# Four cross-attention layers on one core: setup work moved inside layer 0, attention 1's first rows moved into layer 0's FFN, and layer 2's raw weights issued by ScalarE's queue

## The chip, the cores and the metric

The kernel runs on one core of a Trainium2 chip. The core has five engines that work side by side, each with its own instruction stream: TensorE (PE, matrix products and transpositions; its weight loads are shown apart as PEld), VectorE (DVE), ScalarE (ACT), GpSimd (POOL) and SyncE (SP, which here only issues DMAs). An engine runs its instructions in order and waits on semaphores for the others. DMAs move data between HBM and the on-chip memories; the matrix products' results land in PSUM, whose banks the other engines copy out.

The metric is the device time of one execution in microseconds. Three runs of the kernel before gave a median of 1427.58 us.

## What is computed

x has the shape (4, 256, 256), ctx (4, 512, 128), all in fp32. There are four layers, each a cross-attention of x to ctx followed by a feed-forward part; both are added to x. Cut to what matters here:

```
layer 0 attention: q = LN((x Wq + bq) by heads), k = LN((ctx Wk + bk) by heads), 16 heads of 16,
                   a second set of 16 keys from the last rows of ctx (Wkv_dca), softmax each,
                   sum of both contexts, times Wo, plus bo
layer 0 FFN:       64 "arrows" (A: 16 rows each); per token the 4 of the largest norm are routed;
                   out = x W^T + (routed arrows) B + bias
layers 1 to 3 attention: xn = LN(x); 16 query heads of 128, 8 key/value heads of 128,
                   softmax(xn Wq (ctx Wk)^T / sqrt(128)) ctx Wv Wo, masked by mask_BxS2
layer 1 FFN:       8 experts, two per token, plus a shared expert (SwiGLU)
layer 2 FFN:       two experts and a gate
layer 3 FFN:       64 tokens of a sequence are chosen, the rest pass by
```

The kernel folds the weights of the attentions of layers 1 to 3 beforehand: for each head m = Wq Wk^T / sqrt(128) and n = Wv Wo, so that queries are multiplied with ctx directly.

## The kernel before

The batch (B = 4) is the outer loop of each attention; rows are tiled by 128 (P), so a batch has NC = 2 chunks of queries and NK = 4 chunks of keys. x stays on chip in `x_sb[b]` through the whole kernel.

On PE, ACT, DVE and POOL the program's order is written out by hand: within a block each of these engines issues its instructions in the order in which the source emits them. The functions are therefore cut into small steps, and the loops call steps of the next piece of work between the steps of the present one. SP, which isn't in that list, issues DMAs as they come.

**Layer 0's attention** (to about 150 us) goes through b = 0 to 3, and for each batch through i = 0 to 7: four scores of a group of heads (`scores`, L1333, ps L1340), the values of the group before (`values`, L1350), and then `between(b, i)` (L1543), which prepares batch b + 1: its layernorm and projections, the normalisation of q and k by heads (class Scale: the small steps hv L1232, hr L1237 on ACT, he L1241 and pad L1244 on DVE), and their transpositions (`transposed`, L1305: pT L1315 on PE, copies to kT and qT on DVE L1327 and ACT L1329). `between` also holds work that is done once in the kernel:

- `bias_rows` (L1280, two additions on DVE), `bias_columns` (L1288: four tiny matmuls pbrow L1291, a DVE copy L1295) and `output_bias` (L1297: four matmuls pbo L1300, an addition on DVE L1301): they carry the values' bias through Wo into the output's bias `bo0`, which `output0` (L1392) adds; `output0(0)` comes at b = 1, i = 6.
- `score_bound` (L1264): seven DVE operations on one partition, whose result is read only when the kernel decides at its end whether its bounds held.
- the mask: `mf` (L1587, a DVE copy), `pmk` (L1591, one transposition on PE), `mbias` (L1592, DVE), for attention 1.
- `quad` (L1597 to L1601): four DVE operations that make a constant for later attentions.

The values' bias rows lie in a tile `brow` (L1050), loaded by DMA at the start; it has the tag "kT" in the pool w0, two buffers, which the tiles kT of the batches share.

**Layer 0's FFN** (F0, L1658 to L1696, about 150 to 235 us) runs over n = 0 to 7, chunks of 128 rows (b = n / 2). Class Arrows has for each n four steps: `vectors` (paf L1424, ACT copies), `routes` (L1435 to L1453: eight operations on DVE and a product `twof` on POOL), `turned` (puTf L1461 on PE, copies on ACT) and `output` (pyf L1470 and L1474 on PE, ysf L1476 on DVE, the sum into x on POOL). Between them `folding(1, ...)` (L974) is called, eight steps over the loop, each with products pm (L985) and pn (L1001) on PE, scaling and squares on ACT (L993, L996) and a copy n_sb on DVE (L1004). PSUM is one pool here, `ring`, which is closed after the loop; the pool `psum` takes its banks.

`routes` of chunk n + 2 is called at the start of turn n, with one exception: for n = 5 the call stands behind the turn's output and its two fold steps.

**Attention 1** (`attention`, L1719) begins with the layernorm of batch 0's rows, unless it is given as `first_xnT`: `Norm` (L908: statistics on DVE, a power on POOL), `tokens` (L925) and `layernorm_T` (L937: four transpositions pxn, then an ACT copy L940). Then `first_queries` (pq L1803) starts the products.

**Layer 1's FFN** (F1) runs 23 blocks of 128 gathered rows from about 600 to 655 us. The loop over j calls for block j + 2 `gather` (an indirect DMA by POOL) and `turn_in` (pxg L2344 on PE, copy xgT L2346 on ACT), for j + 1 `rise` (pgu L2369 on PE, sigmoids sg L2374 and L2375 on ACT, products gT on DVE) and for j `fall` (pyr L2387). For every second j the two blocks are finished (`last_rows`, L2393) and stored: `yr` (L2398, ACT, three buffers), from which a DMA on SP's queue (L2401) writes `yd` in HBM. Inside this loop the raw weights of attention 2 are loaded by `load_raw` (L958, DMA at L969), a quarter each at the end of j = 1, 5, 9 and 13, held back until the last yr before it (`done["slots"]`). A quarter is four DMAs: 512, 128, 128 and 512 KB. `folding(2, ...)` uses them after the loop.

## Time and profile before

| what | value |
|---|---|
| three runs, median (lowest to highest) | 1427.58 us (1425.8 to 1429.04) |
| profiled execution, its own time | 1426.74 us |
| its span on the core | 1424.9 us |
| mean granted TensorE clock | 0.997 |
| PE busy | 1401.6 us |
| DMA, whole kernel | 46.82 MB, mean 33 GB/s |

The profile page cuts the span into 40 slices of 35.6 us. In the row of PE a 9 is 90% or more of the slice; the row of GB/s shows where transfers crowd: the 18th slice, 605 to 641 us, reaches 217 GB/s:

```
PE   9999999999999999999999999999999999999998
ACT  5667454433433332255443333333454333333331
PEclk9999999999999999999999999999999999999999
GB/s 163 2 1 2 75 75 1 86 27 1 8 0 8 1 8 22 53 217 91 49 56 8 16 1 1 8 1 9 117 106 48 16 1 1 1 1 1 1 1 33
```

Some of the DMA issues (line, queue, count, size of each, median time from issue to landing):

```
wq<-in_L_wqT SPq DMA_DIRECT2D x11, 512.0 KB, 5.1
wo<-in_L_wo SPq DMA_DIRECT2D x11, 512.0 KB, 7.4
yd<-yr SPq DMA_DIRECT2D x23, 128.0 KB, 4.9
```

In a row of a timeline the first number is the start in us from the span's start, the second the time to the end of the group, then engine, line, operation, tiles out<-in, shapes and count; in brackets stands the engine's idle time just before and what ended it.

### The profile page before, as it was taken

The page shows a single profiled execution, that of the slowest core. Times are in us where ns is not written, and L with a number is a line of the kernel's source. Part 1 is how long each engine was busy: PE and PEld are TensorE (multiplying, and loading weights), DVE is VectorE, ACT ScalarE, POOL GpSimd, SP SyncE. Part 2 cuts the span into 40 slices and gives each one's busy share as a digit, 9 for nine tenths or more (in the row PEclk, how much of TensorE's full clock was granted, in tenths as well). Part 3 has the DMA queues.
Part 4 walks back from the last instruction along what each step waited for, and adds up shares of the span by engine and source line. Part 5 has one row for each costly group of instructions (what it writes and reads, how often), then busy time and mean ns, then how long its engine had stood idle before and what let it go on. Part 6 is the DMA issues. An engine that isn't in the chain of part 4 may idle for free. (4 is left out here: it accounts for less than half of the span.)

```text
span 1424.9 us, 20263 instructions
## 1 busy us (share of the span) xinstructions
PE 1401.6 (98%) x7393; PEld 927.0 (65%) x7393; DVE 896.7 (63%) x2012; ACT 590.2 (41%) x1168; POOL 679.2 (48%) x812
## 2 busy tenths in 40 slices
PE   9999999999999999999999999999999999999998
PEld 7566676566556667887555666665985556666666
DVE  6666863666665557554676565648755666575675
ACT  5667454433433332255443333333454433333331
POOL 3322332475655455231566656566214765445560
PEclk9999999999999999999999999999999999999999
DMA  5000220300000000272120000000331000000000
GB/s 163 2 1 2 75 75 1 86 27 1 8 0 8 1 8 22 53 217 91 49 56 8 16 1 1 8 1 9 117 106 48 16 1 1 1 1 1 1 1 33
DMA packets 49449, 46.82 MB, mean 33 GB/s; under 512 B 8281, under 2 KB 45242, under 8 KB 49340
## 3 DMA queue, kind: packets, MB, share of 16 engines
q1 hardware_dynamic: 45740, 37.29, 8.6%
q0 software_dynamic: 2496, 6.82, 1.8%
q8 instruction: 61, 1.00, 0.3%
q10 hardware_dynamic: 1104, 1.31, 0.3%
q14 instruction: 48, 0.39, 0.1%
HBM read 38.60 MB, written 6.82 MB: 32 GB/s over the span
## 5 line engine op out<-in xcount | busy, mean ns | idle before, releaser
L1870 POOL TENSOR_TENSOR half<-pT 128x1024 f32<-128x1024 f32 x93 | 218.2, 2347 | 290.7 <-ACT pT L1854 215.6
L1851 PE MATMUL ps<-qT,cT 128*128 128x512 f32 x768 | 345.6, 593 | 0.0
L1859 PE MATMUL po<-pT,c_sb 128*128 128x512 f32 x768 | 345.3, 592 | 0.0
L1854 ACT ACTIVATE pT<-ps,mbias 128x512 f32<-128x512 f32 x384 | 263.7, 687 | 155.9 <-PE ps L1851 141.6
L1859 PEld LDWEIGHTS po<-pT,c_sb 128*128 128x128 f32 x768 | 145.8, 190 | 183.2 <-issue 183.2
L1851 PEld LDWEIGHTS ps<-qT,cT 128*128 128x128 f32 x768 | 138.9, 190 | 138.4 <-issue 136.5
L1863 ACT COPY oT<-po 128x512 f32<-128x512 f32 x96 | 56.2, 586 | 265.0 <-PE po L1859 265.0
L1906 POOL TENSOR_TENSOR oT<-oT,wide 128x512 f32<-128x512 f32 x90 | 114.3, 1290 | 17.3 <-DVE wide L1905 17.3
L1831 DVE TENSOR_TENSOR qT<-qT,paq 128x128 f32<-128x128 f32 x90 | 25.4, 283 | 94.9 <-ACT qT L1830 94.9
L1344 ACT ACTIVATE pT<-ps 128x512 f32<-128x512 f32 x128 | 65.9, 604 | 32.6 <-PE ps L1340 32.4
L1878 DVE TENSOR_TENSOR half<-half 128x512 f32<-128x512 f32 x96 | 71.6, 746 | 2.7 <-POOL half L1868 2.5
L1831 DVE TENSOR_TENSOR w<-w,pao 128x128 f32<-128x128 f32 x21 | 6.0, 286 | 106.5 <-ACT w L1830 106.5
L1880 DVE STREAM_TRANSPOSE turned<-half 128x512 f32<-128x512 f32 x96 | 68.3, 712 | 6.3
L1821 PE MATMUL paq<-xnT_a,m_sb 128*128 128x128 f32 x360 | 71.3, 280 | 0.0
L1821 PE MATMUL paq<-xx,m_x 128*128 128x128 f32 x360 | 69.6, 275 | 0.0
L1821 PEld LDWEIGHTS paq<-xnT_a,m_sb 128*128 128x128 f32 x360 | 57.3, 192 | 17.2 <-issue 8.7
L1884 DVE TENSOR_REDUCE sums<-turned 128x16 f32<-128x512 f32 x96 | 65.9, 686 | 3.3
L1821 PE MATMUL pao<-n_x,ox 128*128 128x128 f32 x336 | 65.2, 276 | 0.3 <-POOL ox L1747 0.3
L1830 ACT COPY qT<-paq 128x128 f32<-128x128 f32 x90 | 23.9, 265 | 94.1 <-PE paq L1821 94.1
L1905 DVE STREAM_TRANSPOSE wide<-rz 128x512 f32<-128x512 f32 x96 | 62.2, 685 | 0.1
L1834 DVE TENSOR_TENSOR qT<-qT,pbq 128x384 f32<-128x384 f32 x90 | 49.9, 554 | 9.4
L1821 PEld LDWEIGHTS paq<-xx,m_x 128*128 128x128 f32 x360 | 54.7, 192 | 0.0
(454 smaller groups left out, 2589.2 us busy)
## 6 DMA issues: line engine op xcount, KB each, us to landing
wq<-in_L_wqT SPq DMA_DIRECT2D x11, 512.0 KB, 5.1
wo<-in_L_wo SPq DMA_DIRECT2D x11, 512.0 KB, 7.4
yd<-yr SPq DMA_DIRECT2D x23, 128.0 KB, 4.9
w<-in_F_w SPq DMA_DIRECT2D x4, 512.0 KB, 3.6
xd<-xn_f SPq DMA_DIRECT2D x7, 256.0 KB, 2.2
wk<-in_L_wkT SPq DMA_DIRECT2D x11, 128.0 KB, 5.2
wv<-in_L_wvT SPq DMA_DIRECT2D x11, 128.0 KB, 5.6
x_sb<-in_x SPq DMA_DIRECT2D x4, 256.0 KB, 3.1
```

What stands on the lines that cost most here:

```text
L1344: nc.scalar.activation(pT[kp][:, j], ps[j], AF.Exp)
L1821: nc.tensor.matmul(p[:, at, :], lhsT=lhsT, rhs=rhs, start=(k == 0 and at == 0), stop=(k == len(of) - 1 and i == which[-1]),)
L1851: nc.tensor.matmul(ps, lhsT=cT[:, b, k * P : (k + 1) * P], rhs=qT, start=True, stop=True)
L1854: nc.scalar.activation(pT[:, k, :], ps, AF.Exp, bias=mbias[:, b, k : k + 1])
L1859: nc.tensor.matmul(po, lhsT=c_sb[:, b, k, :], rhs=pT[:, k], start=(k == 0), stop=(k == NK - 1))
L1863: done["head"] = nc.scalar.copy(raw, po).ins
L1870: nc.gpsimd.tensor_tensor(half, pT[:, 0:2], pT[:, 2:4], ALU.add)
L1878: nc.vector.tensor_tensor(part, half[:, 0], half[:, 1], ALU.add)
L1880: nc.vector.transpose(turned.rearrange("p f i -> p (f i)"), part)
L1884: nc.vector.tensor_reduce(sums[b, hp // 4][:, hp % 4, :], turned, AX.X, ALU.add)
L1905: nc.vector.transpose(wide, rzs[b, hp // 4][:, hp % 4, :, None].to_broadcast([P, NB, 32]))
L1906: eng.tensor_tensor(outs[b, hp], outs[b, hp], wide.rearrange("p f i -> p (f i)"), ALU.mult)
```

## The change

Four edits are joined.

1. In layer 0's `between`, `bias_rows`, `bias_columns` and `output_bias` go from b = 0, i = 0, 1, 4 to b = 1, i = 0, 1, 2; `score_bound` from b = 0, i = 3 to b = 3, i = 2; the mask from b = 1, i = 0, 1 to b = 3, i = 0, 1; `quad` from b = 1, i = 6 to b = 3, i = 3.
2. In F0 `routes` of chunk 7 is called at its normal turn, at the start of n = 5.
3. Attention 1's first layernorm moves into F0's loop: `Norm` at the end of n = 5, `tokens` at the end of n = 6, `layernorm_T` at n = 7 between the output and the last fold step; `attention(1, ...)` is given the result.
4. `load_raw` takes a queue, and the four loads for layer 2 are issued by ScalarE: 16 DMA instructions that were in SP's stream are in ACT's.

```diff
-    def load_raw(L, i, after=None, tiles=None):
+    def load_raw(L, i, after=None, tiles=None, queue=None):
...
-            dma = nc.sync.dma_start(dst, src[a * P : (a + z) * P, :].rearrange("(h e) d -> e h d", e=P))
+            dma = (queue or nc.sync).dma_start(dst, src[a * P : (a + z) * P, :].rearrange("(h e) d -> e h d", e=P))
...
-            if b == 0:
+            if b == 1:
                 if i == 0:
                     bias_rows()
                 elif i == 1:
                     bias_columns()
-                elif i == 3:
-                    score_bound()
-                elif i == 4:
+                elif i == 2:
                     output_bias()
-            if b == 1:
+            if b == B - 1:
                 if i == 0:
 
                     mf = w0.tile([B * NK, P], F32, tag="hs", name="mf", bufs=1)
...
-                elif i == 6:
+                elif i == 2:
+                    score_bound()
+                elif i == 3:
 
                     nc.vector.tensor_reduce(
...
-            if n + 2 < B * NC and n != 5:
+            if n + 2 < B * NC:
                 arrows[n + 2].routes()
...
+                if n == 7:
+                    first_xnT = layernorm_T(xn1, "a1_0")
                 for _ in range((0, 0, 1, 1, 2, 2, 1, 1)[n]):
                     next(fold)
-                if n == 5:
-                    arrows[7].routes()
...
+            if n == 5:
+                norm = Norm(0, "a1_0")
+            if n == 6:
+                xn1 = norm.tokens()
...
-        attention(1, *mn, after=beside1)
+        attention(1, *mn, first_xnT=first_xnT, after=beside1)
...
                     load_raw(
                         2, 0, done["slots"],
                         (mn[1][:, 8:12, :], mn[0][:, 1, 12:14, :], mn[0][:, 1, 14:16, :], mn[1][:, 12:16, :]),
+                        queue=nc.scalar,
                     )
                 if j in (5, 9, 13):
-                    load_raw(2, j // 4, done["slots"])
+                    load_raw(2, j // 4, done["slots"], queue=nc.scalar)
```

## The prediction

> **What bounds the kernel now.** I read the page's busy table and slices first, then the chain of waits, then TensorE's (PE) timeline for every group with an idle time before it, and last the other engines' timelines around those places.

> ```profile
> span 1424.9 us, 20263 instructions
> PE 1401.6 (98%) x7393; PEld 927.0 (65%) x7393; DVE 896.7 (63%) x2012; ACT 590.2 (41%) x1168; POOL 679.2 (48%) x812
> PE 24%; DVE 1%; POOL 0%; issue 0%
> ```

> PE is busy 98% of the span, no other engine over 65%, and the chain, as far back as it could be followed (a quarter of the span), is PE. So a microsecond put on PE, or a wait of PE removed, anywhere, is a microsecond at the end. PE idles for only 1424.9 − 1401.6 = 23 us. In its timeline these gaps lie where the change works (start, busy, then in brackets the idle time before and what ended it):

> ```profile
> 51.65 1.53 PE L1315 MATMUL pT<-ident,pad 128*128 128x128 f32 x12 [2.08 <-DVE qT L1327]
> 82.92 1.13 PE L1340 MATMUL ps<-qT,kT 16*128 16x256 f32 x10 [1.32 <-DVE qT L1327]
> 227.16 1.09 PE L1461 MATMUL puTf<-ident,twof 128*128 128x128 f32 x8 [1.26 <-POOL twof L1453]
> 235.19 0.63 PE L937 MATMUL pxn_a<-ident,xn_a 128*128 128x128 f32 x4 [0.88 <-DVE n_sb L1004]
> 236.50 3.72 PE L1803 MATMUL pq<-xnT_a,m_sb 128*128 128x256 f32 x16 [0.67 <-ACT xnT_a L940]
> 638.83 1.59 PE L2369 MATMUL pgu<-xgT,we 128*128 128x128 f32 x12 [0.70 <-ACT xgT L2346]
> 649.96 1.59 PE L2369 MATMUL pgu<-xgT,we 128*128 128x128 f32 x12 [1.37 <-ACT xgT L2346]
> ```

> **Part A, layer 0's setup moves to later batches.** The 2.08 us gap in batch 0 ends with VectorE (DVE). Its timeline before it, and ScalarE's (ACT) one row that matters:

> ```profile
> 42.60 0.24 DVE L1267 TENSOR_TENSOR prm<-prm 1x96 f32<-1x96 f32 x1
> ...
> 43.83 0.42 DVE L1301 TENSOR_TENSOR bo<-bo,pbo 128x256 f32<-128x256 f32 x1
> 44.17 0.25 DVE L1241 SCALAR_TENSOR_TENSOR he<-hr 128x96 f32<-128x96 f32 x1
> 45.04 1.76 DVE L1244 TENSOR_TENSOR pad<-qk,hr 128x1536 f32<-128x1536 f32 x1
> ```

> ```profile
> 43.03 0.28 ACT L1237 ACTIVATE hr<-hr 128x96 f32<-128x96 f32 x1
> ```

> From 42.60 to 44.17 DVE does score_bound (seven tiny operations, 1.20 us) and output_bias's addition (0.42), both moved away, while `he` needs only `hr`, ready at 43.31. Behind `he`, DVE is packed to the qT copy that PE awaits at 51.65. Freed, `he` waits for `hr` alone, and this comes earlier by the 0.4 us that PE no longer spends on pbrow (rows at 30.72 and 31.08): 43.31 − 0.4 = 42.9, against 44.17: **−1.24 us**. Bounds: −0.8 if only `hr` as it stood counts, −2.0 if the whole gap closes. The four pbo matmuls (0.96 us of PE to the next issue) leave batch 0 too, but inside that wait, so they bring nothing more there.

> In batch 1 they return on a PE that has no gap before 82.92: pbrow +0.40, pbo +0.96, and the mask's transposition leaves (pmk, −0.23): **+1.12**. They don't shorten the 1.32 us gap, since its DVE chain starts from PE's products. quad's removal from batch 1 (1.08 us of DVE at 83.95) lies behind that gap: 0, at best −0.5. In batch 3 pmk costs PE **+0.23**; the mask's two DVE operations (0.37), score_bound (1.20) and quad (1.08) make 2.65 us of DVE. DVE stands idle for 5.5 us at 135.15–140.71, which hides them; without that cover, 2.65 us would fall on the quotients and projections of batch 3. Sum of A: −1.24 + 1.12 + 0.23 = **+0.1** (−0.9 to +0.6). One uncertainty: brow shares two buffers with the kT tiles, and is now read after batch 1's kT is allocated. If kT1 takes batch 0's buffer instead, its first copy waits for the scores ending at 49.57, about 1 us, inside the wait that ends at 51.65: 0.

> **Part B, routes of the last arrow group at its normal turn.** Before, routes(7) began on DVE at 219.61 and ended on GpSimd (POOL) at 227.1, and PE waited 1.26 us for it. Moved to the start of n = 5, it falls at about 211, where DVE idles (206.7–210.7); ysf(5) behind it comes some 0.9 us later, and PE has the folding's products to do meanwhile. So **−1.26** (−1.43 by the start-to-start distance; −1.0 if ysf's delay shows).

> **Part C, attention 1's first rows into the F0 loop.** The four transpositions pxn_a (0.44 us of issue) are done in either place. Their wait of 0.88 and the 0.67 for the ACT copy behind them fall away, as the last fold's PE work now lies between copy and use. What may be left: the 0.88 was the PSUM bank, which n_sb's copy on DVE (234.35–235.04) frees, and pq, now first in the new banks, may wait for the same. Full −1.74, with that wait kept −0.86: I take **−1.3**. Norm and tokens of these rows ran on DVE and POOL between 170.9 and 183.4; they bring 2.65 us to the stretch of n = 5 and 6, into the 5.4 us of DVE that the late routes leave at 219.61–225.03. If they come in front of an n_sb copy there, PE waits for the copy by up to that much.

> **Part D, 16 DMA issues from SyncE's queue to ScalarE's.** SP has nothing else to do; ACT has. ACT and then PE at the first of the four loads, then the same four issues on SP:

> ```profile
> 607.34 0.84 ACT L2398 ACTIVATE yr<-pyr,wslot 128x256 f32<-128x256 f32 x2 [0.46 <-PE pyr L2393]
> 608.06 0.37 ACT L2346 COPY xgT<-pxg 128x256 f32<-128x256 f32 x1
> ...
> 638.04 0.47 ACT L2398 ACTIVATE yr<-pyr,wslot 128x256 f32<-128x256 f32 x1 [1.75 <-DMA yd<-yr]
> ...
> 649.17 0.47 ACT L2398 ACTIVATE yr<-pyr,wslot 128x256 f32<-128x256 f32 x1 [2.43 <-DMA yd<-yr]
> ```

> ```profile
> 609.49 1.49 PE L2369 MATMUL pgu<-xgT,we 128*128 128x128 f32 x12
> ```

> ```profile
> 608.71 0.45 SPq L969 DMA_DIRECT2D n_sb<-in_L_wqT  x1
> ...
> 610.30 0.47 SPq L969 DMA_DIRECT2D n_sb<-in_L_wo  x1
> ```

> One load takes 610.77 − 608.71 = 2.06 us of its queue. That an issue holds ACT up shows at the kernel's start: three DMAs issued there at 0.79, 1.29 and 1.84 with the table load following at 2.32. So behind the second yr (end 608.18) four issues run to 610.24, xgT to 610.6, and pgu starts at 610.65 in place of 609.49: 1.16 us a load, queued behind it the sigmoids, which still make the fall of the next block. Four loads: **+4.6**. Lower bound 0.4 each, if the issues begin while yr runs; upper 2.1, as SP's third load took 3.0 us with one issue at 1.2. Gained: yr has three buffers and waits twice for a yd store that queues behind the raw weights; on PE that is 0.70 + 1.37 = **−2.07**. Taken in full, since a PE that stalls 1.16 us a load also gives the stores that much more time. Sum of D: **+2.5** (1.6 − 2.07 = −0.5, to 8.4 − 2.07 = +6.3).

> The gathers speak against that gain: on a queue of their own they land 2.75 us after issue, but 5.1 to 6.75 while raw weights run, so another queue is only part of a cure. [...]

> **Sum.** +0.1 − 1.26 − 1.3 + 2.5 = 0.0 on the profiled execution's 1426.74 us (span 1424.9 and 1.8 around it). The three runs have a median of 1427.58, 0.8 above the profiled one, so **1427.6 us**. A change can be told from none here from 0.2%, 2.85 us, on: faster is below 1424.7, slower above 1430.4.

> **Rivals.** (1) *ACT's issues are cheap* (faster): they overlap yr, 0.4 us a load, and with the yd waits gone D is −0.5 and the whole −3.0: 1424.6, or with C in full and A at its better end (−0.4, −0.9) 1423.2. For it: SP's record shows issue, not how long ACT itself stands; against it: the table load at 2.32. (2) *ACT's issue waits* (slower): the four loads run 9.5 us apart and land about 8 us after issue; if an issue on ACT must wait for an earlier landing, or lasts 3 us as SP's third load did, PE stalls 2.1 us a load, D is +6.3, the whole +3.8: 1431.4. It decides from 1.9 us a load on (0.0 + 4 × 0.7 = 2.85). For it: SP's wv issues of 1.19 and 1.16 us; against it: the first two loads show none. (3) *The clock moves.* Between 84 and 88 us the granted clock is 0.57 and PE runs at half pace, 3.4 us long, behind the 1.32 us gap. Such a stretch vanishing or coming behind one of ACT's stalls is ∓1.7 us: 1425.9 or 1429.3. [...]

> **How the numbers follow.** Forecast, with the smaller errors around it, 0.41, own range 1425 to 1430.2; rivals 3 and 4 lie inside and take 0.08 and 0.10 of it. Rival 1, with chains of small gains in A and C: 0.31. Rival 2, with a second half-clock stretch: 0.28. The range: the low end 1426.74 + 0.84 − 4.6 (all low bounds: −0.9, −1.43, −1.74, −0.5) = 1423.0; high end, rival 2 and 1 us more of A and C at their bad ends, 1432.4.

> **What would show it.** The gap at 51.65 down to about 0.9, none before puTf(7) and pxn_a, one at most of 0.9 before pq; in F1 four new gaps of about 1.2 before pgu, ended by xgT, behind four ACT issues, and none at 638.8 and 650. It is wrong if ACT's copies don't come later behind the issues, if batch 1's gap grows by the moved DVE work, or if the folds' DVE copies slip behind Norm and stall PE at 225–235.

## The result and the profile after

In 20 runs each, the changed kernel has a median of 1429.1 us (1426.39 to 1435.69) and the kernel before one of 1428.26 us (1425.62 to 1430.87). The ratio is 1.001 with a 95% interval of 0.9999 to 1.0021: no difference that can be told. The runs of the changed kernel lie in groups that go with the mean granted clock of TensorE: at 0.998 they took 1426.4 to 1427.5 us, at 0.995 to 0.996 1429.0 to 1431.8, at 0.993 (four of the 20) 1435.0 to 1435.7.

The profiled execution took 1427.38 us. The page after, in the same two lines as before:

```profile
span 1425.6 us, 20269 instructions
...
PE 1401.3 (98%) x7393; PEld 926.9 (65%) x7393; DVE 898.4 (63%) x2012; ACT 589.8 (41%) x1168; POOL 679.5 (48%) x812
```

PE is as busy as before and the span 0.7 us longer. What changed is where it waits. PE's timeline of the kernel after, at the places shown of the kernel before (line numbers behind L1600 are some four higher):

```profile
50.71 2.77 PE L1315 MATMUL pT<-ident,pad 128*128 128x128 f32 x12 [1.79 <-DVE qT L1327]
...
84.84 1.13 PE L1340 MATMUL ps<-qT,kT 16*128 16x256 f32 x10 [1.33 <-DVE qT L1327]
...
226.50 1.04 PE L1461 MATMUL puTf<-ident,twof 128*128 128x128 f32 x8
...
234.92 3.69 PE L1807 MATMUL pq<-xnT_a,m_sb 128*128 128x256 f32 x16 [0.88 <-DVE n_sb L1004]
...
607.52 1.59 PE L2373 MATMUL pgu<-xgT,we 128*128 128x128 f32 x12 [1.16 <-ACT xgT L2350]
618.66 1.59 PE L2373 MATMUL pgu<-xgT,we 128*128 128x128 f32 x12 [1.38 <-ACT xgT L2350]
629.63 1.60 PE L2373 MATMUL pgu<-xgT,we 128*128 128x128 f32 x12 [1.21 <-ACT xgT L2350]
641.03 1.60 PE L2373 MATMUL pgu<-xgT,we 128*128 128x128 f32 x12 [1.65 <-ACT xgT L2350]
```

The waits before puTf and before attention 1's transpositions are gone, the one before pq is 0.88 us, the two behind the yd stores are gone, and four new ones stand in the expert blocks, 5.40 us together.

A small wait doesn't tell what it costs, so I matched the matmuls of the two traces one by one and took the difference of their starts (after minus before). Between two places the difference changes by what lies there:

| matmul (start before) | start after minus before | what lies since the row above |
|---|---|---|
| pT 22.76 | +0.30 | start of the kernel |
| pT 51.65 | −0.94 | A in batch 0: −1.24 |
| ps 54.54 | +0.68 | half-clock stretch here, only after: +1.62 |
| ps 66.77 | +1.92 | A in batch 1: +1.24 |
| pxn_a 91.63 | +0.30 | half-clock stretch here, only before: −1.62 |
| pxn_f 130.90 | +0.78 | A in batch 3: +0.48 |
| puTf 227.16 | −0.65 | B: −1.43 |
| pq 236.50 | −1.57 | C: −0.92 |
| pysh 597.46 | −3.28 | half-clock stretch here, only before: −1.7 |
| pgu 649.96 | +0.67 | D: +3.95 |

So the even result of these two profiles is a sum: A +0.5, B −1.4, C −0.9, D +4.0, which makes +2.1; the start of the kernel adds 0.3, and one half-clock stretch that this execution happened to lack takes off 1.7, which leaves the 0.7 us between the spans.

Part A's step worked as the prediction has it: `he` on DVE now waits only for `hr`. The DVE timeline after:

```profile
43.22 0.26 DVE L1241 SCALAR_TENSOR_TENSOR he<-hr 128x96 f32<-128x96 f32 x1 [0.66 <-ACT hr L1237]
```

That is 0.95 us earlier than before (44.17), 1.25 against the start. And kT1 did take batch 0's buffer, as its copy on ACT shows, which now waits for the scores:

```profile
48.97 0.78 ACT L1329 ACTIVATE kT<-pT,cols 128x512 f32<-128x512 f32 x1 [1.22 <-PE ps L1340]
```

It ends at 49.75, inside PE's wait, and costs nothing. ACT's timeline after, at the first load of part D:

```profile
604.05 0.84 ACT L2402 ACTIVATE yr<-pyr,wslot 128x256 f32<-128x256 f32 x2 [0.45 <-PE pyr L2397]
604.92 0.41 ACTq L969 DMA_DIRECT2D n_sb<-in_L_wqT  x1
605.37 0.58 ACTq L969 DMA_DIRECT2D m_sb<-in_L_wkT  x1
605.99 0.55 ACTq L969 DMA_DIRECT2D m_sb<-in_L_wvT  x1
606.58 0.48 ACTq L969 DMA_DIRECT2D n_sb<-in_L_wo  x1
607.10 0.37 ACT L2350 COPY xgT<-pxg 128x256 f32<-128x256 f32 x1 [2.21 <-PE pxg L2348]
```

The four issues run one behind the other from the end of yr, and xgT, ready long before, starts when the last is out. PE waits for it at 607.52. The bracket names pxg, which was done before; what held xgT up stands in the four lines above it.

### The profile page after: what moved, and what is told of

Same layout as the page of the kernel before. It is cut to its first block, busy times and chain, and to the rows that moved or that the text cites. A ratio compares the mean times of both kernels' runs of the same rounds, so it can differ in the third digit from the quotient of the medians.

```text
span 1425.6 us, 20269 instructions
## 1 busy us (share of the span) xinstructions
PE 1401.3 (98%) x7393; PEld 926.9 (65%) x7393; DVE 898.4 (63%) x2012; ACT 589.8 (41%) x1168; POOL 679.5 (48%) x812
```

## The experiments

All were timed in five rounds, 5 to 12 runs each, beside the kernel before on the same chip. "Shift" is the difference of matched matmuls' starts to the profile of the kernel before, as in the table.

| run | edit | median us | ratio, 95% interval |
|---|---|---|---|
| e1_abc_sp | changed kernel, loads back on SP | 1428.12 | 0.999 (0.9975 to 1.0006) |
| e2_d_only | before + D | 1432.17 | 1.0032 (1.0019 to 1.0046) |
| e3_a_only | before + A | 1429.07 | 0.9999 (0.9988 to 1.0009) |
| e4_yr8 | before + eight yr buffers | 1427.25 | 0.999 (0.9981 to 0.9999) |
| e5_d_half | before + half of D's issues | 1429.76 | 1.0011 (1.0001 to 1.0022) |
| e6_d_spread | before + D, one issue a turn | 1428.1 | 0.9992 (0.9976 to 1.0009) |
| e7_best_a | gaining parts | 1421.55 | 0.996 (0.9947 to 0.9974) |
| e8_best_b | the same, fold before output | 1422.27 | 0.996 (0.9947 to 0.9974) |
| e9_after_spread | changed kernel, one issue a turn | 1424.26 | 0.9981 (0.9968 to 0.9994) |
| e10_before_warm | before + idle matmuls | 1432.06 | 1.0024 (1.0013 to 1.0035) |
| e11_best_warm | e7 + idle matmuls | 1429.57 | 1.0001 (0.9989 to 1.0014) |
| e12_best_c | e7 + a copy on ACT | 1418.7 | 0.9947 (0.9934 to 0.9961) |

### The parts by themselves

**e1_abc_sp.**

```diff
-                        queue=nc.scalar,
...
-                    load_raw(2, j // 4, done["slots"], queue=nc.scalar)
+                    load_raw(2, j // 4, done["slots"])
```

> The changed kernel with the raw weights of layer 2 back on SyncE's queue: parts A, B and C alone. Theory (the parts add up, as the two traces show them by the shift of matching matmuls: A +0.5, B -1.43, C -0.92, D +3.9 us): 1.85 us below the kernel before, a ratio of about 0.9987; no idle time of PE before puTf at the last arrows, 0.88 us kept before pq, and in the expert blocks only the two old waits of 0.70 and 1.37 us. Rival (the moves in layer 0 and its FFN are worth nothing, the difference of the two profiles there is the half-clock stretch that fell elsewhere): ratio 1.000, and a profile without that stretch shows no shift at attention 1's first product.

Its profile shows B −1.42 (shift +4.38 at pxn_f, +2.96 at puTf) and C −0.92 (+2.04 at pq), the same as in the changed kernel, and the wait before pq:

```profile
238.54 3.69 PE L1807 MATMUL pq<-xnT_a,m_sb 128*128 128x256 f32 x16 [0.88 <-DVE n_sb L1004]
```

The time alone settles nothing: the interval holds both 0.9987 and 1.000. This execution had three half-clock stretches instead of two, two of them of double length. Of the old yd waits one of 0.42 us is left, so these vary from run to run too. No run was above 1431.8, against four above 1434.9 of the changed kernel. Compared at equal clock, the times do tell: at 0.997 to 0.998 e1 took 1421.9 to 1423.5 us and the changed kernel (at 0.998) 1426.4 to 1427.5, at 0.993 e1 took 1428.6 to 1431.8 and the changed kernel 1435.0 to 1435.7. So D's loss, some 4 to 5 us, stands in both groups, and the group at 1435 us is that loss on top of a low clock. These two kernels weren't timed side by side, but the kernel before had the same median beside each (1428.3 and 1428.26).

**e2_d_only.**

```diff
+                        queue=nc.scalar,
...
-                    load_raw(2, j // 4, done["slots"])
+                    load_raw(2, j // 4, done["slots"], queue=nc.scalar)
```

> The kernel before with only part D: ScalarE issues layer 2's raw weights. Theory (four issues hold ScalarE up for 2.1 us a load and PE for 1.2 to 1.6): four idle times of PE of 1.2 to 1.7 us in the expert blocks, ended by xgT, no wait for yd, 3.9 us above the kernel before, ratio about 1.0027. Rival (the stalls only take the place of waits that the gathers and stores would bring anyway): ratio within 1.0007. If the runs at 1435 us of the changed kernel come from these stalls, they are seen here too, and not in the kernel with parts A, B and C alone.

PE's timeline in the expert blocks:

```profile
610.84 1.59 PE L2369 MATMUL pgu<-xgT,we 128*128 128x128 f32 x12 [1.13 <-ACT xgT L2346]
621.78 1.59 PE L2369 MATMUL pgu<-xgT,we 128*128 128x128 f32 x12 [1.19 <-ACT xgT L2346]
632.70 1.60 PE L2369 MATMUL pgu<-xgT,we 128*128 128x128 f32 x12 [1.15 <-ACT xgT L2346]
643.94 1.59 PE L2369 MATMUL pgu<-xgT,we 128*128 128x128 f32 x12 [1.48 <-ACT xgT L2346]
```

The shift is +0.05 before the first load and +3.48 at 900 us: D costs 3.4 us in the profile, and 1.0032 is +4.6 us (2.7 to 6.6). This is the change's loss. Two of its six runs took 1434.7 us and more, on a median of 1432.2. But such a time doesn't need D: of the 29 runs of the kernel before that were timed beside e5 to e8, two took 1434.25 and 1437.32 us, at clocks of 0.993 and 0.991. None of these executions was profiled.

**e3_a_only.** Only the block in `between` is changed, as in edit 1.

> The kernel before with only part A: layer 0's setup work in later batches. Theory (0.9 to 1.2 us gained in batch 0's wait, 1.4 us of matmuls added on a PE that is full in batch 1, 0.2 in batch 3): 0.3 to 0.5 us above the kernel before, ratio 1.0002 to 1.0004, with 1.8 us of idle time left before batch 1's transpositions. Rival (the shorter DVE chain pays in full): 1.2 us below, ratio 0.9992.

Shift +0.42 at the start, −0.83 at pT 51.65, +0.42 at 91.63 (where both kernels have had one half-clock stretch), +0.89 at 130.90: −1.25 in batch 0, as much back in batch 1, +0.47 in batch 3. The wait left is 1.77 us. The part's own work says +0.5; the time can't tell that from nothing.

### The yd waits and the issues

**e4_yr8.** The store uses a pool that is otherwise used behind the loop:

```diff
-                    yr = fp.tile([P, D], F32, tag="yr", name=f"yr{j}", bufs=3)
+                    if j % 2 == 0:
+                        state["yr"] = backp.tile([P, 2, D], F32, tag="yg", name=f"yr{j}")
+                    yr = state["yr"][:, j % 2, :]
```

> The kernel before with the expert rows yr in eight buffers (four tiles of a pool that is used only later) in place of three; the raw weights stay on SyncE's queue. Theory (ScalarE waits for yd's landing only because yr's buffers run out, so this cures what part D cures, without its issues on ScalarE): the waits of 0.70 and 1.37 us before pgu vanish, 2.07 us below the kernel before, ratio 0.9985. Rival (the gathers, late under the raw weights too, take their place): waits of PE for xg of 0.5 us or more each at the same blocks, ratio 0.9995 to 1.000.

No wait before pgu over 0.24 us is left, and the shift goes from +3.73 at 630 us to +1.24 at 649.96: −2.49. The yd stores near the loads land as late as before (5.2 to 7.3 us behind the issue, before 4.8 to 6.6, in the four of each whose landing the trace gives), and nobody waits for them. The theory holds, at somewhat more than the sum of the two gaps, 2.07.

**e5_d_half.**

```diff
-            dma = nc.sync.dma_start(
+            dma = (queue if queue and z == 4 else nc.sync).dma_start(
```

> The kernel before; of each load's four DMAs ScalarE issues the two large ones (wq, wo), SyncE the two small. Theory (the stall is issue time: four issues of 0.5 us against ScalarE's spare 0.9 us): about 1.0 us of issues a load, so idle times of PE of 0.2 us or less in place of 1.2 to 1.5, and the waits for yd as before or shorter; ratio 0.999 to 1.0005. Rival (ScalarE's issue waits for an earlier transfer to land or for ring space): stalls of 1 us or more stay, ratio 1.002.

PE's and ACT's timelines:

```profile
623.51 1.60 PE L2369 MATMUL pgu<-xgT,we 128*128 128x128 f32 x12 [0.36 <-ACT xgT L2346]
644.17 1.59 PE L2369 MATMUL pgu<-xgT,we 128*128 128x128 f32 x12 [1.05 <-ACT xgT L2346]
```

```profile
642.22 0.48 ACT L2398 ACTIVATE yr<-pyr,wslot 128x256 f32<-128x256 f32 x1 [0.95 <-DMA yd<-yr]
642.72 0.42 ACTq L969 DMA_DIRECT2D wq<-in_L_wqT  x1
643.18 0.52 ACTq L969 DMA_DIRECT2D wo<-in_L_wo  x1
643.74 0.37 ACT L2346 COPY xgT<-pxg 128x256 f32<-128x256 f32 x1 [1.05 <-PE pxg L2344]
```

The stall goes with the issue time: the first three loads shift PE by 0.2 to 0.6 us each in place of 1.3 to 1.5. Half the issues cost less than half, as part of them falls into ACT's spare time. The wait of 1.05 us, at the fourth load, comes of both: yr waits 0.95 us for yd, and then the two issues hold xgT up by another 1.0. Before, a wait of 1.75 us for yd there put 0.70 on PE; so, as an estimate from these rows, the 0.95 alone would have cost PE nothing, and the issues alone what they cost at the other loads. Expected was a little less. The time doesn't decide, as its interval holds both the theory's 1.0005 and the rival's 1.002; the rows of the first three loads do.

**e6_d_spread.** The four DMAs of a load are put into a list, and each turn issues one:

```diff
-                    load_raw(2, j // 4, done["slots"])
+                    load_raw(2, j // 4, done["slots"], steps=steps)
+                if steps:
+                    behind(nc.scalar.dma_start(*steps.pop(0)), done["slots"])
```

> The kernel before; all 16 DMAs are issued by ScalarE, but one at the end of each turn j = 1 to 16 in place of four at the end of j = 1, 5, 9 and 13. Theory (issue time, as above: 0.5 us fits into ScalarE's spare 0.9 us of each turn): no new idle time of PE over 0.2 us, no wait for yd on PE, 2.1 us below the kernel before, ratio 0.9985. Rival (any DMA issue on ScalarE costs PE its time): 16 short stalls that sum to 4 us or more, ratio 1.002 or above.

ACT's timeline at the first load:

```profile
608.24 0.41 ACTq L2501 DMA_DIRECT2D n_sb<-in_L_wqT  x1
608.70 0.37 ACT L2351 COPY xgT<-pxg 128x256 f32<-128x256 f32 x1 [0.48 <-ACT yr L2403]
609.08 0.39 ACTq L2501 DMA_DIRECT2D m_sb<-in_L_wkT  x1
609.73 0.37 ACT L2351 COPY xgT<-pxg 128x256 f32<-128x256 f32 x1
```

Each xgT comes 0.6 us later at most, and PE has no wait before pgu over 0.24 us in the blocks. The shift stays at +0.04 up to 630 us and is −2.46 at 649.96. So the same 16 issues on the same queue gain 2.5 us one at a time and lose 3.4 four at a time. A half-clock stretch at 753 us took 1.6 back in this execution; the ratio's interval holds both 0.9985 and 1.000, and the profile decides for the theory.

**e9_after_spread** is the changed kernel with that same edit.

> The changed kernel with its 16 ScalarE issues spread over the turns j = 1 to 16 instead of four at a time; parts A, B and C as they are. Theory (the bunching of four issues is all that part D costs): A +0.5, B -1.43, C -0.92, the yd waits of about 2.1 to 2.5 gone: some 4.1 us below the kernel before, ratio 0.9971, no idle time of PE over 0.25 us in the expert blocks. Rival (the change's even result is the clock's doing, not the four stalls'): ratio 0.9995 or above.

Span 1419.7 us, shift +0.89 at 130.90, −0.54 at puTf, −1.46 at pq, −5.65 at 649.96; of the last step 1.7 us are a half-clock stretch at 590 us that this execution lacked, and 2.4 the yd waits. With A, B and C untouched, the spreading alone brings the changed kernel clear below the kernel before, by 2.7 us (0.9 to 4.6). The rival falls, if narrowly: its 0.9995 lies just outside the interval, the theory's 0.9971 inside.

### Joining what gains, and the clock

**e7_best_a** keeps B and C, leaves the biases in batch 0 and the mask in batch 1, moves score_bound and quad, and has e4's buffers.

> The parts that gain, together: B, C, of A only score_bound and quad (the biases stay in batch 0, where PE waits anyway, the mask in batch 1), and the yr rows in eight buffers in place of D. Theory by the parts: score_bound -0.8, B -1.43, C -0.92, yr -2.07: 5.2 us below the kernel before, ratio 0.9964. Rival (the matmuls' clock decides: the stretches at half clock come as often): ratio above 0.998.

The ratio 0.996 is −5.7 us. The shift goes from +0.56 at pT 22.76 to −0.25 at pT 51.65 (score_bound, −0.81, though the bias additions stay), and to −5.23 at 649.96, −5.79 in all. In it a half-clock stretch at 52 us that the kernel before lacked (+1.6) and one at 590 us that it had (−1.7) make up for each other. The theory holds, and the clock doesn't decide.

**e8_best_b**, at n = 7:

```diff
-                arrows[n].output()
+                if n != 7:
+                    arrows[n].output()
...
                     next(fold)
+                if n == 7:
+                    arrows[n].output()
```

> As the one before, and at n = 7 the last fold step stands before the last arrows' output in place of behind it, so that the copy of n_sb is done well before attention 1's first product. Theory (pq waits 0.88 us for the bank that this copy frees): the idle time before pq falls to 0.2 us or less, 0.9 us below the one before. Rival (pq waits for whatever the old pool of banks does last, now ysf's addition): 0.5 to 0.9 us stay.

PE's timeline:

```profile
235.63 3.69 PE L1811 MATMUL pq<-xnT_a,m_sb 128*128 128x256 f32 x16 [0.61 <-DVE ysf L1476]
```

The rival was right: pq waits for the last reader of the old pool's banks, n_sb's copy in e7 and ysf's addition here. Nothing is gained: from puTf to pq the shift falls by 0.42 us here and by 0.92 in e7.

**e10_before_warm.** The added matmuls multiply the identity into a tile that nobody reads.

```diff
                 elif i == 7:
+                    if b == 0:
+                        warm(14)
                     transposed(n, range(3, NQK))
...
+                    if (b, hg, kp) == (2, 0, 0):
+                        warm(11)
                     scores(b, hg, pT, kp)
```

> The kernel before with idle matmuls put into two of PE's waits in layer 0 (14 before batch 1's last transpositions, 11 before batch 2's first scores; their product is read by nobody). Theory (the stretches at half clock at 50 to 56 and 84 to 92 us follow these waits, and each costs 1.7 us or more of PE): both waits fall to 0.6 us or less, no granted clock under 0.9 there, 1.5 to 3.5 us below the kernel before, ratio 0.9975 to 0.999, and a narrower spread of the runs. Rival (the stretches come from the small score matmuls around, or the fill only moves them): clock of 0.5 stays in the windows from 50 to 92 us, ratio 0.9995 to 1.0005.

PE's timeline:

```profile
52.62 4.79 PE L1407 MATMUL pwarm<-ident 128*128 128x128 f32 x28 [2.08 <-DVE qT L1327]
```

The fill didn't fill: the whole 2.08 us stand before it, and then it takes 4.8 us of its own. The second one, at 94.99 us, came behind the other wait, which stayed at 1.32 us. A clock of 0.5 stayed too (0.54 and 0.61 in the windows 52 to 54 and 54 to 56 us), as the rival has it; but with both waits unfilled the experiment doesn't tell what brings it. It tells something else: a matmul that needs no data waits as long as the transpositions did. So the wait is for room to write, a PSUM bank of the ring that DVE's qT copy holds; e12 puts that to the test. **e11_best_warm**, the same on e7, lost what e7 had gained (1.0001 against 0.996).

> The parts that gain, together (B, C, score_bound and quad of A, yr in eight buffers), with the same idle matmuls in the two waits as in the kernel before with the fill. Theory (the parts and the clock add up): 5.2 us by the parts and 1.5 to 3.5 us by the clock, ratio 0.994 to 0.9955. Rival (the fill does nothing for the clock): ratio 0.996, as without it.

**e12_best_c** moves that copy:

```diff
-                    if c % 2:
+                    if c % 2 and c != 1:
                         nc.vector.tensor_scalar(dst, src, cols[:, i, 0:1], cols[:, i, 1:2], ALU.mult, ALU.add)
```

> As the first version of the gaining parts together (B, C, score_bound and quad of A, yr in eight buffers), and the second query chunk's copy to qT in layer 0 is done by ScalarE in place of VectorE. Theory (PE's waits of 1.8 us before batch 1's last transpositions and of 1.3 us before batch 2's scores are for the PSUM bank that this copy frees, and the copy stands last in VectorE's chain of quotient, Norm and copy; ScalarE stands idle there): both waits fall to 0.5 us or less, and some 2.6 us more than the version without it are gained, 7.8 us below the kernel before, ratio 0.9945; with the waits gone, the stretches at half clock right behind them are gone or rarer. Rival (ScalarE's exponentials, now 0.8 us later, hold PE up in its place): the sum of PE's waits there stays within 0.8 us of before, ratio 0.996.

PE's timeline where the gap of 2.08 us was:

```profile
48.02 1.20 PE L1340 MATMUL ps<-qT,kT 16*128 16x256 f32 x16
49.15 1.53 PE L1315 MATMUL pT<-ident,pad 128*128 128x128 f32 x12
...
81.88 1.95 PE L1315 MATMUL pT<-ident,pad 128*128 128x128 f32 x8 [1.29 <-DVE y_sb L1400]
```

In batch 0 there is no wait left. In batch 2 the wait of 1.3 us only moved, to one for y_sb, and half clock came behind it as before (0.50 from 82 to 84 us). So half of the theory holds. With 1418.7 us against 1425.97 beside it, this version has the lowest ratio, 7.6 us (5.6 to 9.4) below the kernel before. Its interval overlaps e7's, so what the copy adds is read from the shift: from pT 22.76 to pT 51.65 it falls by 2.99 us, in e7 by 0.81.

What the clock did there is seen in the windows of 2 us (after the busy columns come the granted clock, the DMA share and GB/s). The kernel after:

```profile
50.00:52.00 2.00, 1.29 (x7) 1.29 (x8) 1.58 (x4) 1.69 (x4) 0.70 (x1) 0.70 0.00 0
52.00:54.00 2.00, 2.00 (x15) 1.44 (x18) 1.10 (x2) 0.78 (x1) 0.00 (x0) 0.50 0.00 0
54.00:56.00 2.00, 2.00 (x40) 1.12 (x32) 1.15 (x3) 0.00 (x0) 0.00 (x0) 0.94 0.00 0
```

The version e12:

```profile
50.00:52.00 2.00, 2.00 (x31) 1.12 (x29) 1.19 (x4) 2.00 (x4) 0.92 (x2) 1.00 0.00 0
52.00:54.00 2.00, 2.00 (x28) 1.27 (x28) 2.00 (x4) 0.62 (x2) 0.00 (x0) 1.00 0.00 0
```

After the change, the sum of what the clock lacks, (0.30 + 0.50 + 0.06) × 2 = 1.72 us, at half clock makes a stretch of 3.4 us; in e12 it isn't there. But the kernel before has full clock here as well, in spite of its wait of 2.08 us, so one profile of e12 doesn't show that it stays away.

## Why the prediction was right, and which steps were not

The forecast was no difference at 1427.6 us, and 1429.1 us is within its own range (1425 to 1430.2). The parts, against what was measured:

- **A**, forecast +0.1 (−0.9 to +0.6): +0.5. Batch 0's −1.24 was right to the hundredth in the shift (−1.24), batch 1's +1.12 was +1.24, batch 3's +0.23 was +0.48. There the four scores behind pmk take 1.82 us in place of 1.41; pmk's bank is held until mbias on DVE at 128.96, which may be the reason, but no run took it apart. My sign of success, a gap of 0.9 us, was wrong beside a right sum: PE, too, comes 1 us earlier to the wait when pbo is gone, so 1.79 us are left. I had named this in the working and forgotten it in the list.
- **B**, forecast −1.26 (−1.43 start to start): −1.43. The gap of a row leaves out the tail of the matmul before; the distance of the starts, which the working had as its other end, was the right term.
- **C**, forecast −1.3 between −0.86 and −1.74: −0.92. Taking the middle was the mistake. The row shows PE's wait for n_sb's copy, a bank's wait, and moving the transposition doesn't free the bank; the nearest row was the end with that wait kept, −0.86. In e8, with another reader last, a wait of 0.61 us stays as well.
- **D**, forecast +2.5: +3.4 alone (e2), +3.95 in the changed kernel. The mechanism held, its stall was too small: 1.16 us a load was the term, and PE's starts shifted by 1.3 to 1.5 at the first three loads and by 1.7 to 1.8 at the fourth. I had put the four issues at 2.06 us, as on SP; on ACT, in the changed kernel, xgT started 2.21, 2.44, 2.26 and 2.70 us behind yr's end, as single wk issues took 0.78 (second load) and 1.12 us (fourth). The gain of 2.07 was 2.5 (e4, e6). One reading of the working was off without touching the sum: the load that took 3.0 us on SP was the fourth, the third took 2.8.
- Rival 1 (cheap issues) fell: four in a row stall PE by 1.3 us and more, two by 0.2 to 0.6, single ones not at all. Rival 2 (issues that wait) had a trace of itself in the two long wk issues only. Rival 3 (the clock) was there: one stretch came at 50 us in place of 84, one at 590 us was absent, worth −1.7 in the profile.
- Rival 4 (yd lands as late with the raw weights on another queue, so its waits of 2.07 us stay on PE: 1429.7 us) fell. Behind the raw weights on one queue yd took 4.8 to 6.6 us from issue to landing (before), on a queue of its own 2.3 to 4.5 with the loads four at a time (e2) and 1.8 to 4.1 with them spread (e6), and in the changed kernel no yr waits for it. The gathers' 5.1 to 6.75 us beside the raw weights, which spoke for this rival, didn't carry over to yd; what makes a small transfer late there was not shown.

The two errors of size, C and D, both went the slow way and made 1.9 us (0.4 and 1.5); B's and A's came to 0.2. The sum of the parts is then +2.1 in place of 0.0, still under the 2.85 us that would have been a difference, but with only 0.8 us to spare. That the forecast of no difference held is thus partly luck; e2's timing alone, +4.6, would make D dearer still.

## What to carry to other kernels

Here a DMA issue given to ACT took ACT's time in its own order: 0.41 to 0.63 us for 14 of the changed kernel's 16, 0.78 and 1.12 for the other two. Weigh such a time against the engine's spare time between two waits of the bound engine, and try the issues one at a time: so they gained 2.5 us (e6), four at a time they lost 3.4 (e2). Before moving a transfer for the sake of a wait, ask what the waiter waits for: here ACT waited for one of three buffers, and eight buffers, from a pool that was used only later, cured it without an issue more on ACT. A change that sums to zero may hold gains worth keeping apart: B, C, score_bound and quad of A and the buffers made 0.996, with one copy moved 0.9947.

## What the runs showed of the hardware

```profile
84.00:86.00 2.00, 0.76 (x9) 0.71 (x10) 1.90 (x5) 0.00 (x0) 1.15 (x2) 0.95 0.00 0
86.00:88.00 2.00, 2.00 (x8) 1.35 (x8) 0.48 (x3) 2.00 (x4) 0.72 (x1) 0.50 0.00 0
88.00:90.00 2.00, 2.00 (x16) 1.44 (x18) 1.10 (x2) 0.84 (x2) 0.00 (x0) 0.50 0.00 0
90.00:92.00 2.00, 2.00 (x24) 0.70 (x16) 0.58 (x2) 0.00 (x0) 0.00 (x0) 0.50 0.00 0
```

(0.05 + 3 × 0.50) × 2 = 3.1 us lacking up to 92 us. The window behind it, 92 to 94 us, has 0.84, so 3.4 us are lacking in all, twice the 1.7 of a single one. The distances of the starts repeat: 505.17 us lie between 84.34 and 589.51 us in the kernel before and between 85.81 and 590.98 us in e1, and 34.13 us between 51.68 and 85.81 us in e1. A tenth of the last, 3.413 us, is also the length of a single stretch, and goes 148 times into the first; what sets this step, no run shows. Stretches come here behind waits of only 1.3 to 1.8 us between small score matmuls (1.32 before, 1.79 after, 1.77 in e3), and the one at 589.5 us comes behind 32 matmuls of 46 columns (from 585.50 us on) with no wait at all. That the waits bring the stretches on is not shown. Where the stretches fall differs by profile, and with it the time. The kernel before, e2, e4, e5 and e6 are the same up to 600 us: before, e2 and e6 have stretches at 84.3 to 84.5 and at 589.5 to 589.7 us and none at 52, while e4 and e5 have them at 51.8 to 51.9, at 86.0 and, doubled, at 591 us, and are 2.9 us later by 597 us for it. For the changed kernel's runs the size agrees: a mean clock lower by 0.005 (0.993 against 0.998) is 7 us of lacking clock in 1427, and those runs are 8.5 us longer. That makes a timing of under 3 us a matter of many runs, and the shift of matched starts the finer measure.
